# Routing counts from two products, the last block's two halves finished apart, and an express wait of block reads for all list stores

## The chip, the core and the metric

One core of a Trainium2 chip runs the whole program. The engines are named as the profile names them: PE (TensorE, the matrix products), PEld (the weight loads that belong to the products), DVE (VectorE), ACT (ScalarE), POOL (GpSimd) and SP (SyncE, which here only issues DMAs). The metric is the device time of one execution in microseconds (us), the median of several runs.

## What is computed

The input is x, 8 sequences of 512 tokens with 256 features. A modulation vector of each sequence gives shifts, scales and gates. Then:

```python
h = layernorm(x) * (1 + ca) + sa
x = x + ga * linear_attention(h)          # 16 heads of 16, causal, running sums
h = layernorm(x) * (1 + cb) + sb
x = x + gb * mixture_of_experts(h)

def mixture_of_experts(x):                # 8 experts, 256 -> 1024 -> 256
    probs = softmax(x @ router_w.T)
    topv, topi = top_k(probs, 2)          # two experts a token
    cw = weights of the two, normalised
    h = gelu(x @ w1[e]); y = h @ w2[e]    # only the two chosen matter
    return sum over e of cw[e] * y[e]
```

Everything is float32.

## The kernel before

**Two kinds of work.** For each of the 8 sequences, in chunks of 128 tokens, the attention part makes the normalised rows, the queries and keys, the causal sums and the new x (functions `early`, `middle`, `late`), and the rows that the experts will read (`rows_of`). After a sequence's four chunks `route` chooses each token's two experts. It counts, for each expert, how many earlier tokens chose it, and so knows the place ("slot") of each pair of token and expert in that expert's list. Then POOL stores each row into its slot in DRAM with an indirect DMA (`scatter`, line 963, 8 stores a sequence): these are the list stores. When lists are full enough, `plan` cuts blocks of 128 or 256 rows of one expert from them, as the table `TAKE` says (line 34), and after the last sequence `plan_rest` cuts all the rest.

**A block.** `fetch` issues three DMAs on SP: the expert's two weight matrices (lines 1216 and 1221, 1 MB each) and the block's rows from the lists (line 1227). `turn_rows` transposes the rows; `experts` computes the first layer group by group (`h_ps`), ACT applies the gelu (`g`), and `second` accumulates the second layer in one PSUM tile `y_ps`, which holds both 128-row halves of a block side by side. `finish` multiplies each half by the token's weight and gate on DVE (tile `y`) and has POOL add the half to its tokens' rows in DRAM with an indirect DMA (line 1321), into `acc`, or for the last blocks into the output itself. The last block of all is finished by `all_of` (line 1429), which calls `second` and `finish` once more when no further block follows.

**The order.** The program does not issue its work in the order of the source. Each piece is put into a planner (class `Plan`) with its engine, an estimated duration, a level (a lower one goes first) and what it reads and writes. `Plan.run` plays the work through with these estimates: each engine takes the ready piece of the lowest level. Expert blocks have levels from 1000 upwards, attention and routing lower ones, so that the experts' products fill what attention leaves free. The order that comes out is then issued as it stands, engine by engine; nothing is reordered on the chip. So an estimate that changes can change the order of other work, too. A group of products (`L.group("PE", us)`) is one piece, and its result counts as ready when the whole group is done.

**What the change touches.** In `route` (line 884): `is_in` holds 1 where an expert is among a token's two, for the four chunks of 8 experts each (128 x 32). The PSUM tile `at_ps` gets, by one product with the matrix `earlier`, the count of earlier tokens of the same chunk, and by four products with a matrix of ones the counts of the earlier chunks:

```python
for c in range(NC):
    product(
        at_ps[:, (c + 1) * E : (NC + 1) * E].rearrange("p (c e) -> p c e", e=E),
        ones, is_in[:, c, :].unsqueeze(1).to_broadcast([P, NC - c, E]),
        start=False, stop=(c == NC - 1), skip_group_check=True,
    )
```

DVE then makes the slots from it (`at`, `where`, `slot`) and adds the totals to `count`, from which `plan` and `plan_rest` work. In `second` and `finish` the halves of a block are one group and one piece of POOL's work. In `route`, `plan` and `plan_rest` the list `q.scatters` holds the stores of the one sequence just routed; a block's read waits for those.

Of the kernel before, what the change touches and what calls it, by code (L numbers as in the profile page):

```python
# [18 lines left out]
P = 128  # L19
# [319 lines left out]
def kernel(  # L339
# [60 lines left out]
    gathered = []  # L400
    added = []
    copied = []

    def apart(inst, others, why):
        for o in others:
# [478 lines left out]
    def route(q):  # L884
# [72 lines left out]
        dve(V.tensor_reduce, where, first, us=0.21, axis=AX.X, op=ALU.add)  # L957
        dve(V.tensor_copy, slot, where)
        dve(V.tensor_add, count, count, at_ps[:, NC * E : (NC + 1) * E])
        q.scatters = []  # L960

        def scatter(c, j):
            s = nc.gpsimd.indirect_dma_start(  # L963
                out=slots, out_offset=IndirectOffsetOnAxis(ap=slot.now()[:, c, j : j + 1], axis=0),
                in_=row.now()[:, c, :], in_offset=None,
                bounds_check=NONE - 1, oob_is_err=False,
            )
            apart(s, scattered + cleared, "a slot is of one pair of token and expert")
            apart(s, gathered, "blocks that are read are full by then")
            scattered.append(s)  # L970

        L.level += LEVEL["scatter"]
        for c in range(NC):
            for j in range(2):
                q.scatters.append(
                    L.do(
                        "POOL", 1.29, lambda c=c, j=j: scatter(c, j), r=[slot, row], landing=2.0,
                        mb=0.27,
                    )
                )  # L980
                q.scatters[-1].indirect = True


    def spans(small, n, tag):
# [294 lines left out]
            )  # L1279
        return block, w1_sb, w2_sb, xT, cw, to, r  # L1280

    def second(y_ps, w2_sb, nt, group, n_groups, each, g, level):

        L.level = level
        with L.group("PE", 0.433 * each * nt):
            for t in range(nt):
                for i in range(each):
                    product(
                        y_ps[:, ts(t, D)], g[:, i * nt * P + t * P : i * nt * P + (t + 1) * P],
                        w2_sb[:, each * group + i, :],  # L1290
                        start=(group == 0 and i == 0 and t == 0),
                        stop=(group == n_groups - 1 and i == each - 1), skip_group_check=True,
                    )

    def finish(block, cw, to, r, y_ps):
# [20 lines left out]
        def add():  # L1316
            halves = []
            for t in range(nt):
                if t:
                    nc.gpsimd.memset(between, 0.0)  # L1320
                s = nc.gpsimd.indirect_dma_start(  # L1321
                    out=out.rearrange("b s d -> (b s) d") if block.at_end else acc,
                    out_offset=IndirectOffsetOnAxis(ap=to.now()[:, t : t + 1], axis=0),
                    in_=y.now()[:, t, :], in_offset=None, compute_op=ALU.add,
                    bounds_check=TOK - 1 if block.at_end else TOK + 2 * P - 1,
                    oob_is_err=nt == 2 or not block.at_end,
                )
                apart(s, halves, "a token comes to an expert once")
                behind(s, added[-1:], "one addition to a token after the other")
# [3 lines left out]
            added.extend(halves)  # L1333

        X.adds.append(
            L.do("POOL", 1.85 * nt, add, r=[to, y], after=after, landing=2.0, mb=0.13 * nt)
        )
        X.adds[-1].indirect = True

    X.stores = []  # L1340

# [58 lines left out]
    for b in range(B):  # L1400
        if b not in xs:
            L.level = 4 * b - 12
            load_x(b, after=[X.stores[b - XS]] if b >= XS else ())
        L.level = 4 * b + LEVEL["open"]
        q = seqs[b] = open_(b, modded)
        for c in range(NC):
            for part, does in (("early", early), ("middle", middle), ("late", late)):
                L.level = 4 * b + c + LEVEL[part]
                does(q, c)
            L.level = 4 * b + c + LEVEL["rows"]  # L1410
            rows_of(q, c, modded)
# [90 lines left out]
```

## Time and profile before

| | us |
|---|---|
| median of 3 runs | 821.01 |
| the runs | 820.64, 821.01, 824.59 |
| the profiled execution | 827.9 |
| its span, first to last instruction | 826.2 |
| PE busy | 792.2 (96%) |
| weight loads busy | 658.3 (80%) |
| DVE busy | 378.0 (46%) |
| POOL busy | 320.6 (39%) |
| ACT busy | 284.3 (34%) |
| mean granted clock of TensorE | 0.985 |

All durations of instructions come from the one profiled execution. Its time is 1.7 us more than its span, and 6.9 us more than the median. In the page's 40 slices DVE is 70% busy or more from the second slice to about the twentieth (to some 400 us), and then a tenth; PE is at 80 to 90% and more in all but the first and last slices. So the program has an attention stage, in which both engines are loaded, and an expert stage, in which PE is nearly alone.

Each product of float32 matrices appears in the trace as two weight loads and two MATMUL instructions, so the 40 products on `at_ps` appear as 80 of each. Nearly all instructions bear line 220, the line of the planner's helper; they are told apart by the names of their tiles.

### The profile page before, as it was taken

What the parts mean: (1) busy time and instruction counts of PE and PEld (TensorE: products, weight loads), DVE (VectorE), ACT (ScalarE), POOL (GpSimd) and SP (SyncE); (2) the same over time, 40 slices, a digit from 0 to 9 for tenths busy, and PEclk for the clock granted to TensorE, in tenths of its full rate; (3) what the DMA queues carried; (4) which work ended last, traced back from release to release, by engine and by line L of the source; (5) the groups of instructions that cost most, each with busy time, mean ns of one, the idle gap of its engine ahead of it and who ended that gap; (6) DMA issues with size and microseconds to landing.
All of it is one profiled execution on the core that took longest, in us unless ns stands there. A gap on an engine that the chain in (4) does not pass through costs nothing. (4 is left out here: it accounts for less than half of the span.)

```text
span 826.2 us, 15967 instructions
## 1 busy us (share of the span) xinstructions
PE 792.2 (96%) x5998; PEld 658.3 (80%) x5998; DVE 378.0 (46%) x1290; ACT 284.3 (34%) x617; POOL 320.6 (39%) x477
## 2 busy tenths in 40 slices
PE   6899989999998999999999999999999999999995
PEld 3567657767786878789888888888988889898884
DVE  4588978888986888777263010111011111111000
ACT  2546444446464475552232122212221212222120
POOL 4734374637383364726138331312221232120133
PEclk9899998999998999999999999999999999999998
DMA  7320183964664353738579966766776878678932
GB/s 232 105 53 27 59 241 126 344 144 123 199 175 123 115 188 116 225 125 237 173 229 295 302 206 190 233 184 206 236 229 191 259 218 243 178 227 297 322 65 27
DMA packets 95167, 154.27 MB, mean 187 GB/s; under 512 B 6632, under 2 KB 69736, under 8 KB 94960
## 3 DMA queue, kind: packets, MB, share of 16 engines
q1 hardware_dynamic: 79680, 125.22, 48.5%
q0 software_dynamic: 15408, 28.00, 13.4%
q8 instruction: 49, 0.80, 0.4%
q14 instruction: 30, 0.25, 0.1%
HBM read 120.19 MB, written 37.20 MB: 191 GB/s over the span
## 5 line engine op out<-in xcount | busy, mean ns | idle before, releaser
L220 PE MATMUL h_ps<-xT,w 128*128 128x256 f32 (+1 forms) x1280 | 257.0, 351 | 2.6 <-issue 2.6
L220 PE MATMUL y_ps<-w,g 128*128 128x256 f32 x1072 | 253.7, 380 | 0.0
L220 PEld LDWEIGHTS h_ps<-xT,w 128*128 128x128 f32 x1280 | 216.3, 195 | 26.1 <-issue 3.2
L220 PEld LDWEIGHTS y_ps<-w,g 128*128 128x128 f32 x1072 | 200.2, 190 | 26.3 <-issue 0.8
L220 ACT ACTIVATE g<-h_ps 128x512 f32<-128x512 f32 x134 | 80.0, 597 | 309.0 <-PE h_ps L220 308.9
L1321 POOL DMA_INDIRECT acc<-y,to x57 | 90.2, 1582 | 243.8 <-DVE y L220 198.2
L220 DVE SCALAR_TENSOR_TENSOR y<-y_ps,cw,r 128x256 f32<-128x256 f32 x67 | 30.0, 480 | 154.6 <-PE y_ps L220 154.5
L220 DVE TENSOR_TENSOR sm<-s_ps,causal 128x512 f32<-128x512 f32 x128 | 82.3, 681 | 12.5 <-PE s_ps L220 12.5
L963 POOL DMA_INDIRECT slots<-row,slot x64 | 65.1, 1017 | 36.4 <-issue 13.1
L220 PE MATMUL qk_ps<-wqkv_sb,hT 128*128 128x512 f32 x128 | 65.1, 633 | 1.1 <-ACT hT L220 1.0
L220 DVE TENSOR_TENSOR cwe<-r,is_of_rest 128x16 f32<-128x16 f32 (+1 forms) x21 | 3.6, 174 | 132.6 <-DMA r<-slots 124.8
L220 POOL TENSOR_TENSOR f<-f,t 128x512 f32<-128x512 f32 x32 | 43.0, 1345 | 52.6 <-DVE t L220 41.5
L220 PEld LDWEIGHTS s_ps<-qT,kT 32*128 32x128 f32 x1024 | 32.6, 186 | 11.4 <-issue 7.3
L220 PE MATMUL s_ps<-qT,kT 32*128 32x128 f32 x1024 | 39.5, 284 | 1.5 <-ACT logits L220 0.7
L220 PEld LDWEIGHTS qk_ps<-wqkv_sb,hT 128*128 128x128 f32 x128 | 24.0, 202 | 20.3 <-issue 14.3
L220 PE MATMUL v_ps<-wqkv_sb,hT 128*128 128x256 f32 x128 | 36.2, 408 | 2.0 <-ACT hT L220 1.9
L220 PE MATMUL oT_ps<-sm,vz 128*32 128x128 f32 x1024 | 36.8, 276 | 1.3 <-DVE sm L220 1.2
L1321 POOL DMA_INDIRECT out_dram<-y,to x10 | 15.6, 1559 | 52.7 <-DMA out_dram<-acc 22.7
L220 POOL TENSOR_SCALAR mv_f<-mv_f 128x1 f32<-128x1 f32 x32 | 9.9, 310 | 64.8 <-DVE mv_f L220 59.3
L220 PE MATMUL a_ps<-wo,oT 128*128 128x256 f32 x128 | 33.6, 385 | 0.5 <-DVE sm L220 0.4
L220 ACT COPY xT<-x_ps 128x512 f32<-128x512 f32 (+1 forms) x40 | 20.6, 515 | 35.1 <-PE x_ps L220 34.8
L220 PEld LDWEIGHTS oT_ps<-sm,vz 128*32 128x32 f32 x1024 | 26.9, 109 | 6.7 <-DVE sm L220 3.2
(227 smaller groups left out, 1000.4 us busy)
## 6 DMA issues: line engine op xcount, KB each, us to landing
w<-in_w_dram SPq DMA_DIRECT2D x80, 1024.0 KB, 5.9
r<-slots SPq DMA_DIRECT2D x27, 521.0 KB, 7.0
row<-modd SPq DMA_DIRECT2D x8, 512.0 KB, 9.7
acc<-x SPq DMA_DIRECT2D x8, 512.0 KB, 3.7
out_dram<-acc SPq DMA_DIRECT2D x8, 512.0 KB, 9.0
x<-in_x_dram SPq DMA_DIRECT2D x7, 512.0 KB, 7.6
r<-slots SPq DMA_DIRECT2D x13, 260.5 KB, 8.7
mod<-modd SPq DMA_DIRECT2D x8, 384.0 KB, 6.3
```

What stands on the lines that cost most here:

```text
L220: return method(now(out), *[now(a) for a in args], **{k: now(a) for k, a in kw.items()})
L963: s = nc.gpsimd.indirect_dma_start(out=slots, out_offset=IndirectOffsetOnAxis(ap=slot.now()[:, c, j : j + 1], axis=0), in_=row.now()[:, c, ...
L1321: s = nc.gpsimd.indirect_dma_start(out=out.rearrange("b s d -> (b s) d") if block.at_end else acc, out_offset=IndirectOffsetOnAxis(ap=to.n ...
```

## The change

- `route`: DVE makes a second copy of `is_in`, called `up_to`, and adds up its chunks in place (one tensor_single_scalar and three tensor_add of 128 x 8 a sequence). The four products with `ones` become one product with `up_to`. The planner's estimate of the group goes from 1.05 to 0.45 us.
- `second` and `finish` get a flag `apart_`, set in `all_of` alone: the last block's last group of products becomes two groups, one for each half; DVE's product for a half follows that half's group, and each half's addition is a piece of POOL's work of its own that needs its own half of `y` alone. For other blocks the parts of `y_ps` are now named to the planner, in one group as before.
- A block's read names as its predecessors the list stores of all sequences so far (the list `scatters`), no longer those of the last sequence alone. Before, the older ones were declared independent of it.

```diff
@@ route
         dve(V.tensor_single_scalar, is_in, rank, 2.0, op=ALU.is_lt)
+        up_to = small([P, NC, E], "up_to")
+        dve(V.tensor_single_scalar, up_to, rank, 2.0, op=ALU.is_lt)
+        for c in range(1, NC):
+            dve(V.tensor_add, up_to[:, c, :], up_to[:, c - 1, :], up_to[:, c, :])
         at_ps = early_bank(f"at_ps_{b}")
-        with L.group("PE", 1.05):
+        with L.group("PE", 0.45):
             product(at_ps[:, : NC * E], earlier, is_in ...)
-            for c in range(NC):
-                product(
-                    at_ps[:, (c + 1) * E : (NC + 1) * E].rearrange("p (c e) -> p c e", e=E),
-                    ones, is_in[:, c, :].unsqueeze(1).to_broadcast([P, NC - c, E]),
-                    start=False, stop=(c == NC - 1), skip_group_check=True,
-                )
+            product(
+                at_ps[:, E : (NC + 1) * E], ones, up_to.rearrange("p c e -> p (c e)"),
+                start=False, stop=True, skip_group_check=True,
+            )
...
-        q.scatters = []
...
-                q.scatters.append(
+                scatters.append(
@@ second
-        with L.group("PE", 0.433 * each * nt):
-            for t in range(nt):
+        for halves in [[t] for t in range(nt)] if apart_ else [range(nt)]:
+            with L.group("PE", 0.433 * each * len(halves)):
+                for t in halves:
...
-                        y_ps[:, ts(t, D)], g[...]
+                        y_ps[:, ts(t, D)].of(t), g[...]
@@ finish
-                V.scalar_tensor_tensor, y[:, t, :].of(t), y_ps[:, ts(t, D)], cw[:, t, :],
+                V.scalar_tensor_tensor, y[:, t, :].of(t), y_ps[:, ts(t, D)].of(t), cw[:, t, :],
...
-        X.adds.append(
-            L.do("POOL", 1.85 * nt, add, r=[to, y], after=after, landing=2.0, mb=0.13 * nt)
-        )
-        X.adds[-1].indirect = True
+        for which in [[t] for t in range(nt)] if apart_ else [range(nt)]:
+            first = which[0] == 0
+            X.adds.append(
+                L.do(
+                    "POOL", 1.85 * len(which), lambda w=which, f=first: (add_first if f else add)(w),
+                    r=[to] + [y[:, t, :].of(t) for t in which], after=after if first else (),
+                    landing=2.0, mb=0.13 * len(which),
+                )
+            )
+            X.adds[-1].indirect = first
@@ the loop over sequences, and what follows it
-            blocks = plan(b, q.scatters)
+            blocks = plan(b, list(scatters))
...
-    blocks, others, more_i = plan_rest(q.scatters)
+    blocks, others, more_i = plan_rest(list(scatters))
...
-        second(*X.pending)
-        finish(*X.ending)
+        second(*X.pending, apart_=True)
+        finish(*X.ending, apart_=True)
```

More of the change, by code (lines that the diff above doesn't have):

```diff
@@ L402 @@
     copied = []
+    scatters = []
     def apart(inst, others, why):
@@ L970, in scatter @@
             scattered.append(s)
+            return s
         L.level += LEVEL["scatter"]
@@ L980, in route @@
                 )
-                q.scatters[-1].indirect = True
+                scatters[-1].indirect = True
     def spans(small, n, tag):
@@ L1280, in turn_rows, with second, finish @@
         return block, w1_sb, w2_sb, xT, cw, to, r
-    def second(y_ps, w2_sb, nt, group, n_groups, each, g, level):
+    def second(y_ps, w2_sb, nt, group, n_groups, each, g, level, apart_=False):
         L.level = level
-        with L.group("PE", 0.433 * each * nt):
-            for t in range(nt):
[L1287 to L1292, printed above, removed]
-                    )
-    def finish(block, cw, to, r, y_ps):
+        for halves in [[t] for t in range(nt)] if apart_ else [range(nt)]:
+            with L.group("PE", 0.433 * each * len(halves)):
+                for t in halves:
+                    for i in range(each):
+                        product(
+                            y_ps[:, ts(t, D)].of(t),
+                            g[:, i * nt * P + t * P : i * nt * P + (t + 1) * P],
+                            w2_sb[:, each * group + i, :],
+                            start=(group == 0 and i == 0 and t == 0),
+                            stop=(group == n_groups - 1 and i == each - 1), skip_group_check=True,
+                        )
+    def finish(block, cw, to, r, y_ps, apart_=False):
         n, nt = block.n, block.nt
@@ L1314, in finish, with add @@
         after = X.adds[-2:] + X.stores[-1:] + (X.copies or [])
-        def add():
-            halves = []
-            for t in range(nt):
+        halves = []
+        def add(which):
+            made = []
+            for t in which:
                 if t:
@@ L1328, in add @@
                 apart(s, halves, "a token comes to an expert once")
-                behind(s, added[-1:], "one addition to a token after the other")
+                behind(s, before_, "one addition to a token after the other")
                 if block.at_end:
@@ L1332, in add, with add_first @@
                 halves.append(s)
-            added.extend(halves)
-        X.adds.append(
-            L.do("POOL", 1.85 * nt, add, r=[to, y], after=after, landing=2.0, mb=0.13 * nt)
-        )
-        X.adds[-1].indirect = True
+                made.append(s)
+            if which[-1] == nt - 1:
+                added.extend(halves)
+            return made
+        before_ = []
+        def add_first(which):
+            before_.extend(added[-1:])
+            return add(which)
+        for which in [[t] for t in range(nt)] if apart_ else [range(nt)]:
[6 more added lines that the diff above has]
+                )
+            )
+            X.adds[-1].indirect = first
     X.stores = []
```

## The prediction

> **What bounds the kernel now.** I first read the busy shares on the page, then one row for each stretch of the span, to see where PE is full and where it isn't.
>
> ```profile
> PE 792.2 (96%) x5998; PEld 658.3 (80%) x5998; DVE 378.0 (46%) x1290; ACT 284.3 (34%) x617; POOL 320.6 (39%) x477
> ```
>
> ```profile
> 60.00:100.00 40.00, 37.85 (x468) 28.15 (x467) 37.02 (x98) 21.04 (x55) 14.02 (x18) 1.00 0.12 38
> 100.00:140.00 40.00, 35.79 (x337) 26.40 (x332) 33.82 (x123) 17.08 (x44) 24.76 (x40) 0.91 0.57 175
> 140.00:180.00 40.00, 38.41 (x453) 29.64 (x452) 31.92 (x87) 20.66 (x53) 21.29 (x32) 1.00 0.85 246
> 180.00:220.00 40.00, 39.35 (x432) 31.32 (x430) 35.22 (x122) 22.75 (x52) 24.09 (x36) 1.00 0.56 167
> 220.00:260.00 40.00, 39.01 (x436) 30.11 (x434) 30.95 (x114) 20.60 (x50) 21.62 (x33) 1.00 0.60 162
> 260.00:300.00 40.00, 37.37 (x362) 31.31 (x361) 30.35 (x102) 19.46 (x43) 22.19 (x35) 0.91 0.42 139
> ...
> 430.00:817.00 387.00, 387.00 (x1907) 342.23 (x1906) 53.87 (x251) 79.30 (x136) 102.43 (x138) 1.00 0.74 222
> ```
>
> The columns after the stretch are its length and the busy us of PE, PEld, DVE, ACT and POOL, then the granted clock and the DMA share. From 430 to 817 PE is busy all the time: 387.00 of 387. From 100 to 300 it idles 40 - 35.79 + 1.59 + 0.65 + 0.99 + 2.63, about 10 us in all, and the waits view names no single cause (the longest is 2.6 us). The experts' products fill what attention leaves. So the end is, to a few us, PE's work plus PE's idle time plus a tail: PE work taken out anywhere shortens the end, unless idle time takes its place. The chain of waits shows only the last addition on POOL and tells nothing of this.
>
> The price of the products on `at_ps` is read from the timeline of the weight loads at the last sequence's route, where PE is full on both sides:
>
> ```profile
> 424.04 1.70 PEld L220 LDWEIGHTS y_ps<-w,g 128*128 128x128 f32 x8
> 425.76 0.41 PEld L220 LDWEIGHTS at_ps<-is_in,earlier 128*128 128x128 f32 x2
> 426.09 0.97 PEld L220 LDWEIGHTS at_ps<-is_in,ones 128*128 128x128 f32 x8
> 426.98 1.60 PEld L220 LDWEIGHTS h_ps<-xT,w 128*128 128x128 f32 x8
> ```
>
> The reader is to see starts, not durations: five products (ten loads) hold the stream from 425.76 to 426.98, 1.22 us. Eight loads span 0.97, each lasts 0.192, so they start every (0.97 - 0.19) / 7 = 0.111 us. The moving matrix has 8 to 32 columns here, and the loads set the pace.
>
> **The change, part by part.** *Three products fewer a route.* Six load-and-product pairs x 0.111 = 0.67 us, x 8 routes = 5.3 us of PE. The other way, from the eight groups' whole stretches (1.11, 1.80, 1.43, 1.14, 1.32, 1.21, 1.32, 1.22, sum 10.55 for 80 pairs), six tenths of them are 6.3 us, but 1.80 lies partly in a stretch of half clock. I take 5.3. The one product that stays has 32 moving columns, as the widest of the four had.
>
> *Four DVE instructions more a route.* A tensor_single_scalar of 128 x 32 like `is_in` (176 ns) and three additions like `count` (152 ns), 0.63 us a route, 5.1 us in all. They depend on each other; dependent small instructions of this kind start 0.21 us apart (`red` at 421.11, 421.33, 421.54), so the chain to the products grows by up to 0.84 us, while the group that follows is 0.67 us shorter: the slots come 0.2 us later at worst. From the end of `is_in` to the first load of `at_ps` 1.40, 0.12, 0.26, 0.68, 1.27, 0.11, 0.86 and 2.34 us pass today; in four of eight the longer chain lies under a wait for PE, or nearly (0.86 is just enough). What hides DVE's time is the experts' backlog on PE. With that cover gone (PE behind DVE in each route) it costs 5.1 us. From below: nothing, where DVE waits for PE anyway (`x` for `a_ps` 24.2 us, `f` for `qk_ps` 12.6). DVE is densest around the routes: in the 8 us after the starts of five of the eight (96:104, 182:190, 225:233, 279:287, 327:335) it is busy 8.00 of 8, and PE idles 0, 0.65, 0.46, 0 and 0. By those five rows PE idles 1.1 us in 40 where DVE is full, so adding 5.1 us of DVE should cost little; I take 1.0 us, about a fifth, for this and for the new order together.
>
> *The new order.* The planner's estimates change, so other pieces may change places. PE has some 11 us of idle time left from the first route on. A new order can win part of that or lose as much; I count it at nothing with 2.5 us to either side, by the size of the longest single gap.
>
> *The wait for all stores.* An older sequence's stores were issued on POOL's queue before the new one's, and those the read already waits for; in the waits view SP stands at line 853 for `slots<-row,slot` (37.5 us, 6 times) earlier still, since the row tile is reused. The last store waited for is the same, so no read moves. What can grow is the number of waits. At the end of the program SP passes pairs of satisfied waits every 0.06 us; four such pairs for each of 40 reads make at most 10 us of SP. Behind a read stand the next block's weight loads and row load, the stores to `acc` and the loads of x; but SP has this to hide it:
>
> ```profile
> SPq L1216 <- PE h_ps L220: 216.4, 32, 19.4
> SPq L1221 <- PE y_ps L220: 96.5, 27, 4.6
> ```
>
> SP waits 216 us in total for PE to free first-layer weights, and PE has no wait for `r` at all. I take nothing. Without that cover a late block costs at most a read's 7.0 us. POOL issues as many stores and additions as before, ACT is not touched.
>
> *The tail.* The last half-block's products, DVE's two multiplications and POOL's two additions are in series:
>
> ```profile
> 813.70 3.43 PEld L220 LDWEIGHTS y_ps<-w,g 128*128 128x128 f32 x16
> ...
> 817.57 0.88 DVE L220 SCALAR_TENSOR_TENSOR y<-y_ps,cw,r 128x256 f32<-128x256 f32 x2 [11.21 <-PE y_ps L220]
> 818.33 1.55 POOL L1321 DMA_INDIRECT out_dram<-y,to  x1 [8.63 <-DVE y L220]
> 819.32 0.60 POOL L1320 MEMSET between<- 1x1 f32 x1
> 820.19 1.56 POOL L1321 DMA_INDIRECT out_dram<-y,to  x1 [0.27 <-POOLq L1453]
> ```
>
> The two multiplications take 0.48 each and 0.88 together, so the second starts 0.40 after the first. The first addition need no longer wait for it: 0.40 us. If DVE could also start when half of the last eight pairs is done (4 x 0.215 = 0.86 us), it would be 1.26 us; the second addition follows 1.86 us behind the first in any case, and its data come in time. No row here shows DVE reading a half of a PSUM tile while PE writes the other. Here the Trainium skill, page "PSUM — Partial Sum Buffer", section "PSUM bank collisions raise a hardware error", speaks against the change: two engines may not be in one bank at once, and the guard has to be by bank, not by address. `y_ps` is 512 float32 wide, one bank by that page. The second half's products come straight behind the first's on PE, so a guarded DVE still starts after both. By the rule 0.40, without it 1.26; I take 0.40.
>
> **The sum.** -5.3 + 1.0 + 0 - 0.4 = -4.7 us. On the profiled execution: 827.9 - 4.7 = 823.2. That execution is 6.9 us above the median, and the stretches show why it may be:
>
> ```profile
> 125.40:132.20 6.80, 5.66 (x70) 4.30 (x69) 6.20 (x25) 3.56 (x10) 2.19 (x3) 1.00 0.44 158
> 132.20:139.00 6.80, 6.80 (x29) 6.18 (x29) 6.49 (x30) 3.14 (x7) 2.62 (x5) 0.50 0.11 42
> ...
> 255.10:261.90 6.80, 4.52 (x58) 2.64 (x56) 3.17 (x9) 4.42 (x13) 2.40 (x5) 1.00 0.29 94
> 261.90:268.70 6.80, 5.92 (x28) 5.95 (x29) 4.38 (x8) 2.51 (x3) 2.94 (x3) 0.50 0.20 60
> ```
>
> Twice after the start PE had half its clock for 6.8 us, each worth about 3.4 us; two make 6.8. I read the two faster runs as having none of them and 824.59 as having one. Against the median the forecast is 821.0 - 4.7 = 816.3.
>
> **The rivals.** *The gain is filled by new idle time.* PE runs ahead sooner, and in the attention stage then waits for DVE, which has 5.1 us more to do and is full around the routes. Against it: the backlog, and the route of the last sequence lies where DVE is nearly idle. All of 5.1 us on the path gives 821.0 - 5.3 + 5.1 - 0.4 = 820.4; half gives 817.9.
>
> *Slower: the attention stage falls into half clock.* Place: the stretches from 84 to 270 in which PE is thin. With less PE work there and a denser DVE, more of them could be granted 0.50. Price: 3.4 us each. It decides from three more such stretches in the median run: 816.3 + 10.2 = 826.5. The skill, page "TensorE: Matmul & The Clock Gate", section "HAM oscillation — how this bites in real kernels", puts the rule as no idle gaps of PE above about 3.4 us. By it this rival is impossible, as PE's longest gap there is 2.6 us, and the sum stands. The rows say otherwise: half clock followed stretches with 5.66 and 4.52 of 6.80 busy and no gap over 2.6. But an earlier thin stretch, 84.41 to 91.24, with 5.30 us busy kept full clock, so the rows give no threshold either. The rows decide: possible, but three at once are unlikely, since 0.67 us less in one stretch of forty is little.
>
> *A lucky order.* The planner's new order also removes about 4 us of the 11 us of idle time: 812.3.
>
> *The change doesn't do what it says.* For the stores' wait I already take that as true. For the tail it would cost 0.4 us.
>
> **How the numbers follow.** A difference below 0.5%, 4.1 us, can't be told from none here: faster means below 816.9, slower above 825.1. The forecast as summed (814 to 818): 0.60; filled by idle time or by a single half-clock stretch (818 to 822): 0.23; three half-clock stretches or an order that loses as much: 0.09; a lucky order: 0.08. Of the first, four fifths are below 816.9, since the doubtful term (1.0 us for DVE) can also be nothing: 0.49 + 0.08 = 0.57 faster; 0.34 within; 0.09 slower. The range 811.5 to 822.0 leaves out the slow rival and a luckier order, with no more than 2 in 10.
>
> **What would show it.** Right: `at_ps` with 32 loads, groups of 0.4 to 0.6 us; PE's busy time lower by 5 us, its idle time from 100 to 430 up by 1 us or less; first addition of the last block 0.4 us closer to the last product, not 1.26; SP's waits for PE still above 200 us. Wrong: waits of PE for `sm`, `row` or `f` that grow by more than 3 us; a wait of PE for rows; or a different number of 0.50 stretches, which would move the profiled time by 3.4 us each.

## The result, and the profile after

| | before | after |
|---|---|---|
| median, us | 820.89 (22 runs, 817.48 to 825.51) | 824.71 (22 runs, 820.64 to 826.97) |
| ratio of after to before | | 1.0037, 95% interval 1.0021 to 1.0052 |
| the profiled execution, us | 827.9 | 825.43 |
| its span, us | 826.2 | 823.7 |
| its mean granted clock | 0.985 | 0.984 |

The kernel became slower by 0.37%. That is less than the half per cent below which the prediction saw no change, but the forecast of 816.3 and its range up to 822.0 are missed, and the sign is wrong. (Ratios stand here as they were recorded, with their intervals; a quotient of two medians can differ from them by some 0.3%.) The two profiled executions say the opposite of the medians: after is shorter by 2.5 us. Both happen to have nearly the same clock. So what can differ between the medians and not between these two profiles is how often an execution is granted the full clock.

First the busy time of the changed kernel, from its page:

```profile
PE 787.6 (96%) x5950; PEld 651.9 (79%) x5950; DVE 386.2 (47%) x1322; ACT 286.4 (35%) x619; POOL 317.1 (38%) x476
```

PE has 24 products fewer (48 MATMULs and as many loads) and 4.6 us less work. The weight loads of the last route, from the timeline of after, show where it went (start, duration, instruction):

```profile
433.06 0.41 PEld L220 LDWEIGHTS at_ps<-is_in,earlier 128*128 128x128 f32 x2
433.39 0.30 PEld L220 LDWEIGHTS at_ps<-up_to,ones 128*128 128x128 f32 x2
433.74 0.30 PEld L220 LDWEIGHTS h_ps<-xT,w 128*128 128x128 f32 x2
```

Four loads hold the stream for some 0.67 us where ten held it for 1.22. Over the eight routes the stretches are 0.92, 0.54, 0.68, 0.87, 0.76, 0.36, 0.44 and 0.67 us, 5.24 in place of 10.55, so 5.31 us less.

The stretches of the attention stage (length; busy us of PE, PEld, DVE, ACT, POOL; granted clock; DMA share and GB/s):

```profile
100.00:140.00 40.00, 36.05 (x368) 26.86 (x367) 34.17 (x124) 17.34 (x45) 23.45 (x39) 0.91 0.51 170
...
260.00:300.00 40.00, 39.11 (x440) 30.88 (x439) 32.52 (x114) 21.95 (x55) 19.49 (x31) 1.00 0.49 152
300.00:340.00 40.00, 36.29 (x391) 27.79 (x393) 31.40 (x104) 17.51 (x42) 16.12 (x25) 0.91 0.44 112
```

The stall that before had after 255 is gone, and another of the same kind stands at 300 to 340. All gaps of over 60 ns in which neither PE nor its loads are busy, after 20 us, add up to 17.7 us before and 20.0 after: 2.3 us of the 5.3 are given back as idle time.

What that stall is, the timeline of after shows:

```profile
319.04 0.17 DVE L220 TENSOR_TENSOR cwe<-r,is_of 128x8 f32<-128x8 f32 x1 [3.52 <-DMA r<-slots]
...
319.29 0.68 DVE L220 TENSOR_TENSOR sm<-s_ps,causal 128x512 f32<-128x512 f32 x1
...
320.03 1.91 PE L220 MATMUL oT_ps<-sm,vz 128*32 128x128 f32 x26 [2.79 <-DVE sm L220]
```

`cwe` is an instruction of 0.17 us that makes the weights of a later expert block from that block's rows. It stands at the head of DVE's queue, its rows are not there, and DVE idles 3.52 us with it. The attention's `sm` is ready behind it and can't pass; PE waits 2.79 us for `sm`. Before has a like picture at 257.8, where `cwe` waits 4.88 us; PE's gap of 2.63 us follows at 260.2, and its row names no releaser. Half clock comes behind the stall, here in after at two places:

```profile
128.10:131.50 3.40, 1.20 (x13) 0.63 (x7) 1.21 (x6) 1.34 (x5) 0.39 (x1) 0.99 0.58 190
131.50:134.90 3.40, 3.40 (x18) 3.40 (x17) 3.40 (x16) 1.86 (x3) 0.00 (x0) 0.50 0.02 5
...
312.40:319.20 6.80, 4.83 (x54) 2.85 (x47) 2.83 (x6) 2.89 (x8) 1.83 (x4) 1.00 0.96 306
319.20:326.00 6.80, 5.97 (x38) 4.84 (x39) 5.31 (x15) 1.55 (x5) 1.26 (x1) 0.50 0.03 11
```

Each thin stretch is granted the full clock, and the one behind it, in which PE is busy again, half. A third half-clock stretch of after, from 117.8 to 121.2, follows one in which PE was busy for 6.18 of 6.90 us, so a long gap is not needed. Between 100 and 430 us both profiles have 13.6 us at half clock.

The tail in after:

```profile
811.36 3.62 PE L220 MATMUL y_ps<-w,g 128*128 128x256 f32 x16
815.01 0.88 DVE L220 SCALAR_TENSOR_TENSOR y<-y_ps,cw,r 128x256 f32<-128x256 f32 x2 [11.21 <-PE y_ps L220]
815.77 1.56 POOL L1329 DMA_INDIRECT out_dram<-y,to  x1 [8.62 <-DVE y L220]
```

From the start of the multiplications to the first addition 0.76 us pass, exactly as before (817.57 to 818.33). The tail gained nothing.

And SP's queue still waits for PE, in the view of its waits (us in all, times, longest):

```profile
SPq L1220 <- PE h_ps L220: 206.7, 32, 20.6
```

### The profile page after: what moved, and what is told of

The parts are those of the page before. It is cut to its first block, busy times and chain, and to the rows that moved or that the text cites. A ratio compares the mean times of both kernels' runs of the same rounds, so it can differ in the third digit from the quotient of the medians.

```text
span 823.7 us, 15905 instructions
## 1 busy us (share of the span) xinstructions
PE 787.6 (96%) x5950; PEld 651.9 (79%) x5950; DVE 386.2 (47%) x1322; ACT 286.4 (35%) x619; POOL 317.1 (38%) x476
## 5 line engine op out<-in xcount | busy, mean ns | idle before, releaser
L220 PE MATMUL h_ps<-xT,w 128*128 128x256 f32 (+1 forms) x1280 | 254.0, 348 | 1.0 <-ACT xT L220 0.5
L220 PEld LDWEIGHTS h_ps<-xT,w 128*128 128x128 f32 x1280 | 213.3, 192 | 24.9 <-issue 0.8
```

The costliest lines, as they stand in the source:

```text
L220: return method(now(out), *[now(a) for a in args], **{k: now(a) for k, a in kw.items()})
```

## The experiments

Times are told as ratios to before, timed on the same chip. The kernels e5 to e8, and e9, e10, e12 and e13, ran on two chips where every kernel, before and after alike, took some 48 us longer; there only ratios are read. "Late" below means that the small DVE instructions that need a block's rows (`cwe`, `cw`, `to`), for the blocks of the attention stage, stand just ahead of their first reader.

**e1: the new counts in before's order.** All five DVE instructions and both products bear before's estimates, so that the planner gives the order of before.

```diff
-        dve(V.tensor_single_scalar, is_in, rank, 2.0, op=ALU.is_lt)
+        with L.group("DVE", 0.15 + 0.00104 * is_in.free):
+            ...is_in, up_to and the three additions as in after
         with L.group("PE", 1.05):
             ...the two products of after
```

> The new counts (two products, four more DVE instructions a route) issued in exactly the order of the kernel before; the tail and the stores' wait as before. Theory ORDER (the loss comes from the planner's new order, the new counts by themselves save about 5 us of PE): about 816, ratio to before 0.993 to 0.996; PE idle time from 20 to 430 within 1.5 us of that of before. Rival DVE (the four DVE instructions a route, on a full DVE, cost more than the products save): 823 to 825, ratio above 1.002.

Measured: 824.13 us, ratio 1.0011 (0.9991 to 1.0032). The counts alone bring nothing in the old order. Apart from the counts' own instructions every engine has the same sequence as in before, so the two profiles can be matched load by load. At 437 us the PE of e1 is 7.1 us ahead. But 3.9 of it are won from 128 to 140 and 4.9 from 256 to 270: there before has its two half-clock stretches, and at the second place a stall of 2.6 us; this execution has neither half clock, and a stall of 1.5. Outside these places e1 is 1.7 us behind before. At five routes (near 96, 182, 224, 279 and 326) a lead of 0.2 to 0.7 us appears and is lost again within 5 us; they are the five behind which DVE is busy for 8.00 of 8 us in before. At the last two (near 375 and 426), where it is busy for 7.17 and 6.77 of 8, 0.65 and 0.67 us stay. PE's waits for DVE's `sm` and `row` show where it goes (us in all, times, longest), in before

```profile
PE rt_ps L220 <- DVE row L220: 1.9, 3, 1.1
PE oT_ps L220 <- DVE sm L220: 1.2, 6, 0.3
PE rt_ps L220 <- DVE sm L220: 1.0, 2, 0.6
PE a_ps L220 <- DVE sm L220: 0.4, 1, 0.4
```

and in e1

```profile
PE rt_ps L220 <- DVE row L220: 2.4, 4, 1.1
PE oT_ps L220 <- DVE sm L220: 2.1, 7, 0.8
PE rt_ps L220 <- DVE sm L220: 1.8, 4, 0.6
PE a_ps L220 <- DVE sm L220: 1.6, 3, 0.7
```

together 4.5 and 7.9 us. From 437 to 462, where the last sequence hands over to the experts, e1 loses another 4.3 us:

```profile
444.77 0.17 DVE L220 COPY to<-r 128x2 int32<-128x2 int32 x1 [10.58 <-DMA acc<-y,to]
...
445.81 1.72 PE L220 MATMUL y_ps<-w,g 128*128 128x256 f32 x4 [2.35 <-issue]
```

Again a small DVE instruction (`to`, the tokens' places) heads the queue, now until an addition to `acc` has landed, and the multiplication that frees `y_ps` stands behind it. Half clock for 3.4 us follows.

**e2: the old counts in after's order.** The five products stay; the planner is told of after's estimates.

```diff
+        up_to = small([P, NC, E], "up_to")
+        L.do("DVE", 0.15 + 0.00104 * up_to.free, lambda: None, r=[rank], w=[up_to])
+        for c in range(1, NC):
+            L.do("DVE", 0.15 + 0.00104 * E, lambda: None, r=[up_to], w=[up_to])
-        with L.group("PE", 1.05):
+        with L.group("PE", 0.45) as counts:
+            counts.reads.append(up_to)
```

> The old five products and no DVE instruction more, but issued in the order that the changed kernel has (the planner is told of the new durations and of four pieces of DVE work that issue nothing); the tail and the stores' wait as before. Theory ORDER: slower than before by what the change lost plus what its products saved, 827 to 830, ratio 1.007 to 1.011; DVE again stands before a late block's rows near 130 and near 319, and PE with it. Rival DVE: as before, ratio 0.998 to 1.002.

Measured: 830.96 us, ratio 1.0090 (1.0058 to 1.0123). Its products and DVE's instructions are those of before, and apart from the counts every engine has the sequence of after (with it come two table loads more on ACT and one memset fewer on POOL). With the old counts this order costs 0.9%, 7.4 us. DVE stands before the rows of a block for 5.33 us at 323, and PE 4.50 us with it, where after's stall at 319 took 2.79. After holds the same order and the new counts, at 1.0037: the counts save 0.5%, 4.4 us, in this order, though the two were not timed side by side (with e16 below it is 0.8%).

**e3: the tail and the stores' wait alone.**

```diff
-            blocks = plan(b, q.scatters)
+            blocks = plan(b, list(scatters))
...
+        second(*X.pending, apart_=True)
+        finish(*X.ending, apart_=True)
```

> The change without its counts: the last block's halves apart and the reads' wait for all stores, five products as before; no engine's order differs from before. Theory ORDER and rival DVE: no difference, ratio 0.998 to 1.002; the first addition of the last block again begins 0.76 us after the first half's multiplication, so the tail gives nothing. Rival WAIT (the express wait delays the reads): 823 to 825, ratio above 1.002, and reads that land later than before.

Measured: 824.01 us, ratio 0.9990 (0.9961 to 1.0020): nothing. The first addition again follows 0.76 us behind the multiplications' start. PE, DVE and POOL do the same instructions with the same number of waits as in before; of the 40 reads of rows four have another number of waits.

These runs gave something else. The program hardly differs from before, and its 14 runs lie apart: six at a mean granted clock of 0.995 with 818.2 to 819.2 us, eight at 0.985 to 0.989 with 823.5 to 827.5. So runs of one program lie some 6 us apart, and the clock goes with the time. The section on the prediction uses this.

**e4: after, with the rows' instructions late and the modulation's loads behind the reads.**

```diff
+    def move(order):
+        ...each of cwe, cw, to of an attention-stage block: just ahead of its first reader
+        ...each load of mod that stands on SP just ahead of a read of rows: behind it
+        return order
+        L.order = move(L.order)
```

> The changed kernel with two moves in the issued order: the three small DVE instructions that need a block's rows stand as late as their users allow (attention-stage blocks only), and two modulation loads on SP stand behind the row reads instead of ahead of them. Theory ORDER, in its form that a late row read at the head of an in-order queue is what thins PE out and brings half clock: DVE's waits for rows before 430 go from 5.7 us to below 1, PE's longest gap after 100 falls below 1.5 us, the half-clock stretches near 131 and 319 are gone, 816 to 820, ratio to before below 1.000. Rival DVE: as the changed kernel, ratio 1.002 to 1.005.

Measured: 823.47 us, ratio 1.0003 (0.9981 to 1.0024). The stall at 319 is gone. (A half clock of 3.4 us remains near 330, behind 4 us in which PE is busy for 2.04 with no gap over 0.73.) But the load of `mod` that was moved is now what is late:

```profile
128.76 0.69 DVE L220 TENSOR_TENSOR wo<-wout_sb,mod 128x512 f32<-128x512 f32 x1 [3.31 <-DMA mod<-modd]
...
129.93 2.07 PE L220 MATMUL s_ps<-qT,kT 32*128 32x128 f32 x26 [3.28 <-DVE x L220]
```

One late transfer was exchanged for another at the same place.

**e5: after, late only.** The first half of that edit.

> The changed kernel with one move alone: the small DVE instructions that need a block's rows (cwe, cw, to) as late as their users allow, for the attention-stage blocks; SP's order as in the changed kernel. Theory HEAD OF QUEUE (a small instruction that waits for a DMA holds an in-order engine, PE goes thin, half clock follows): DVE waits for rows before 430 fall from 5.7 to below 0.5 us, PE's gap of 2.8 near 317 and the half clock at 319 go; the gap near 129 stays, since PE itself waits for the rows there. Time below the changed kernel by 2 to 6 us: 819 to 823, ratio to before 0.998 to 1.002. Rival CHANCE (half clock comes whatever the queues do): as the changed kernel, 1.002 to 1.005.

Measured: 873.12 us, ratio 1.0041 (1.0021 to 1.0060), where after gave 1.0037 on another chip: no gain seen. (A later run beside after on one chip corrects this.)

**e6: e1 with more buffers for `to`.**

```diff
-        to = L.tile(pb, [P, 2], "to", f"to_{n}", 3, I32)
+        to = L.tile(pb, [P, 2], "to", f"to_{n}", 6, I32)
```

> The new counts in the old order, and the tile of the rows' targets (to) has six buffers, not three, so that its copy on DVE need not wait for an older addition to land. Theory HEAD OF QUEUE: DVE's wait of 10.6 us for an addition near 434 to 445 and PE's gap of 2.3 at 443 go; the 7 us that the new counts are ahead by there are kept up to the slack of the first block of the rest (4 us), so PE then runs 4 to 7 us ahead of before; 816 to 819, ratio 0.994 to 0.998. Rival HANDOVER (the rest's first rows land when the last stores do, whatever PE does): PE waits for rows near 460 instead, ratio 0.999 to 1.003.

Measured: 877.88 us, ratio 1.0093 (1.0069 to 1.0118; 6 runs). Slower, not faster. The waits of `to` for an addition, 27.9 us in all in e1, are gone in this profile; PE's longest gap at the handover is now 3.7 us, near 499, behind ACT's `g`. So that the wait of `to` is what loses time there is not shown. What the buffers do by themselves is not known, since e1 did not run on this chip.

**e7: before, late.** The `move` above on before, without the loads of `mod`.

> The kernel before with the same one move (cwe, cw, to as late as their users allow, attention-stage blocks), five products, nothing else. Theory HEAD OF QUEUE: DVE's wait of 4.9 us for rows at 258 goes, and with it PE's gap of 2.6 at 260 and the half clock at 262: 815 to 819, ratio 0.993 to 0.998. Rival CHANCE: as before, 0.999 to 1.002.

Measured: 865.79 us, ratio 0.9950 (0.9928 to 0.9971; 7 runs). Faster than both kernels.

**e8: e6, late.**

> The new counts in the old order with both remedies: six buffers for the targets, and cwe, cw, to late for the attention-stage blocks. Theory HEAD OF QUEUE: the best of all, 813 to 817, ratio 0.990 to 0.996, no half clock between 100 and 430. Rival HANDOVER: not below e7, since what is gained ahead of 430 is lost at the first block of the rest: ratio 0.996 to 1.000, with a wait of PE for rows near 460.

Measured: 869.47 us, ratio 0.9992 (0.9963 to 1.0020). Late is worth 0.9992/1.0093, 1.0%, on top of e6; yet e8 stays 0.4% behind e7, before with late and the old counts.

**e9 and e10: the planner told that rows land after 6 us, not 2,** in after and in before. The reads of rows take 7.0 to 8.7 us from issue to landing on the pages of both kernels.

```diff
-        L.do("SP", 0.6, rows, r=[block.slot], w=[r], after=block.seen, landing=2.0, mb=0.26 * nt)
+        L.do("SP", 0.6, rows, r=[block.slot], w=[r], after=block.seen, landing=6.0, mb=0.26 * nt)
```

> The changed kernel with one number more: the planner is told that a block's rows land 6 us after their issue, not 2 (measured from issue to landing: 7.1 median, 5.6 to 10.9), so it makes another order again. Theory ESTIMATE (the order holds engines at rows that have not landed since the planner expects them too early): DVE's waits for rows before 430 below 1 us, no gap of PE above 1.2 us between 100 and 430 that ends with the landing of rows, below the changed kernel of the same chip by 3 to 7 us, ratio to before 0.993 to 0.999. Rival CHANCE (one order is as good as another, only luck decides): ratio anywhere from 1.000 to 1.006.

> The kernel before with the same one number (rows land after 6 us, not 2), five products. Theory ESTIMATE: DVE's wait of 4.9 at 258 goes; below before by 1 to 5 us, ratio 0.994 to 0.999, and e9 below it by 3 to 5 us, what the products save. Rival CHANCE: 0.998 to 1.005 and no fixed distance to e9.

Measured: after 883.0 us, ratio 1.0149 (1.0111 to 1.0188); before 874.34 us, 1.0042 (1.0027 to 1.0057). The theory that a truer estimate would mend the order fell in both. DVE's waits for rows before 430 us did become short (1.8 us in e9, where after has 3.0 on that chip, and 0.7 in e10), but the time rose; PE's longest waits there are now for ACT's `oT`, 4.6 and 7.8 us. A changed estimate makes a new order for everything.

**e12 and e13: after again, and e7 again,** on the same chip as these two.

> The changed kernel itself once more, on the chip of the other kernels here, as their common measure. Both theories: ratio to before 1.002 to 1.005; hardly a run with a mean clock of 0.993 or more, where before has a quarter of its runs there.

> The kernel before with cwe, cw, to as late as their users allow (as in e7), once more on this chip. Theory HEAD OF QUEUE: ratio 0.993 to 0.998 as in e7, no PE gap of 2.6 near 260 and no half clock there. Rival CHANCE: e7 was luck of its chip, 0.999 to 1.002.

Measured: after 875.59 us, 1.0062 (1.0042 to 1.0082); before with late 868.32 us, 0.9969 (0.9952 to 0.9985). After is slower than before here too, and before with late faster.

**e14 to e16: the order's price without waits for rows.** The kernel with old counts in after's order and late as well (e14), after with late (e15, the kernel of e5) and after (e16), all on one chip, where before takes 823.8 us.

> Before with its five products a route, issued in the order of after (as e2), but cwe, cw and to of the attention stage's blocks stand on DVE just ahead of their first reader, as in e7. Theory ROWS (the order's price of 0.9% in e2 is the wait of DVE for rows in the attention stage): the ratio falls from 1.009 to that of e7, 0.995 to 0.998. Theory SPREAD (most of the order's price lies elsewhere: the handover at 430 to 465, PE's waits for other things): ratio 1.004 or more.

> e5 once more, beside after on the same chip. Theory ROWS: faster than after by 0.4% or more, near 0.999 of before. Theory SPREAD: within 0.2% of after, 1.003 to 1.006 of before, as e5 had it. Its ratio to e14 is the worth of the counts in one order without waits for rows: 0.994 if the three products fewer are on the path there, 1.000 if what is saved is lost again.

> After itself, as the measure for e14 and e15 on this chip: 1.0037 to 1.0062 of before by its other runs.

Measured: e14 825.79 us, 1.0033 (1.0015 to 1.0052); e15 820.09 us, 0.9971 (0.9954 to 0.9988); e16 823.74 us, 1.0009 (0.9994 to 1.0025). e14 lies between what the two theories expected: set against e2, on another chip, late takes away 0.57% of 0.9%, and something is left. Between e14 and e15 the counts differ (and the tail and the stores' wait, which brought nothing in e3): 0.9971/1.0033 = 0.9938, 5.1 us. And late does help after, by 0.38%; e5 had been compared with after on another chip.

**e11: the tail with two PSUM banks.** Before, the last block's second half in a bank of its own, its products a group of their own.

```diff
-        with L.group("PE", 0.433 * each * nt):
...
+        for part in parts:
+          with L.group("PE", 0.433 * each * len(part)):
...
+            y_ps = [y_ps, late_bank(f"y2_ps_{n}") if final else y_ps]
```

> Before with only the last block's halves changed: two groups of products in two PSUM banks, each multiplied when its own group is done. Theory BANK (in after DVE waits for both halves since they share a bank): DVE's first multiplication starts about 0.86 us earlier against the last product than in before, so its start lies ahead of the last product's end; the first addition follows it by 0.5 to 0.8 us, and the end of the span comes about 0.9 us nearer to the last product. Theory QUEUE (DVE or POOL is bound by something else, such as its own start-up): nothing moves.

Measured, in the timeline of this kernel:

```profile
810.44 3.62 PE L220 MATMUL y_ps<-w,g 128*128 128x256 f32 x16
813.23 0.48 DVE L220 SCALAR_TENSOR_TENSOR y<-y_ps,cw,r 128x256 f32<-128x256 f32 x1 [10.35 <-PE y_ps L220]
813.99 1.55 POOL L1323 DMA_INDIRECT out_dram<-y,to  x1 [7.76 <-DVE y L220]
814.09 0.48 DVE L220 SCALAR_TENSOR_TENSOR y<-y_ps,cw,r 128x256 f32<-128x256 f32 x1 [0.38 <-PE y_ps L220]
```

The last products end at 814.06. DVE's first multiplication starts 0.83 us ahead of that, where in before it starts 0.04 behind; the first addition comes 0.07 ahead, where it came 0.80 behind. The addition is 0.87 us nearer to the last product, and that is the 0.86 us that the prediction had worked out for a DVE that needn't wait for the second half. By the semaphores in the traces the wait is one of the program: in before and after only the last of the 16 MATMULs signals to DVE, here also the last one of the first half, which ends at 813.19. That fits the theory of the bank; but the edit gives the second half another tile and another bank at once, and does not tell the two apart.

**e17 and e18: both repairs in after, and e7 once more,** on one chip with before at 821.93 us.

> After with cwe, cw and to of the attention stage's blocks just ahead of their first reader (e15), and the last block's second half in a PSUM bank of its own (e11). By e15 0.9971 of before, and 0.87 us less by e11: 0.996. If the tail's gain is lost (a second bank that something else wanted), 0.997.

> Before with cwe, cw and to late, alone (e7), on the same chip as e17. If the planner's order costs more than waits for rows (e14 at 1.0033 against 0.995 to 0.997 here), this stays at 0.995 to 0.997, level with e17, and the counts' 5 us are what the order takes back. If e7 owed its gain to the slower chip it ran on, 0.999 or more, and then the waits are the order's whole price.

Measured: e17, after with late and two banks, 820.43 us, 0.9982 (0.9966 to 0.9997); its first addition again comes 0.07 us ahead of the last product's end, but 0.1% is too little to see in the ratio. e18, before with late: 816.74 us, 0.9934 (0.9910 to 0.9957; 6 runs at a clock of 0.993 to 0.995). It is the fastest kernel of the study, 0.66% under before, with the same instructions in another order. With late in both orders and the old counts, after's order costs 1.0033/0.9934 = 1.010 (about 1.007 to 1.013 from the two intervals; 1.008 and 1.006 with e7 and e13 in place of e18), much as without late. So waits for rows are an item of their own, which before and after both pay, and not the price of the order.

What the order loses with the old counts and late, the stretches of the two kernels show at one place. First e14, in after's order, then e18, in before's:

```profile
100.00:140.00 40.00, 36.26 (x366) 26.87 (x362) 32.88 (x115) 17.26 (x45) 22.67 (x37) 0.91 0.53 163
...
119.00:122.40 3.40, 3.40 (x7) 1.83 (x6) 3.31 (x7) 0.36 (x1) 2.19 (x5) 0.56 0.44 138
...
129.00:132.40 3.40, 1.15 (x8) 0.75 (x7) 3.40 (x13) 1.43 (x4) 0.02 (x1) 0.98 0.55 197
132.40:135.90 3.50, 3.50 (x20) 3.50 (x19) 0.28 (x1) 2.08 (x3) 0.00 (x0) 0.53 0.02 5
```

```profile
100.00:140.00 40.00, 36.41 (x393) 27.78 (x392) 35.69 (x127) 19.21 (x51) 25.72 (x43) 1.00 0.55 190
```

PE is busy for nearly the same time in both, but in e14 at half clock for some 7 us of it. In the thin stretch from 129.0 to 132.4 PE waits 1.75 us for the first block's rows. SP's queue and the product in after, which has the same order there:

```profile
119.07 0.34 SPq L656 DMA_DIRECT2D mod<-modd  x1
...
120.95 0.35 SPq L1231 DMA_DIRECT2D r<-slots  x1
```

```profile
130.41 0.41 PE L220 MATMUL x_ps<-ident,r 128*128 128x128 f32 x2 [1.74 <-DMA r<-slots]
```

In after's order the load of the next sequence's `mod` stands ahead of the first block's read of rows on SP and issues only at 119.07; the read follows at 120.95. In before the `mod` load comes behind it (121.51), and the read issues at 118.54, in before with late at 116.82. But this sets e14 apart from e18, and not after from before: before's own row for 100 to 140 us has 0.91 too, with half clock from 132.2 to 139.0 behind no gap above 0.7 us, although its read stands ahead of `mod`. The rest of the price is spread: over the whole span PE's gaps of over 60 ns add up to 20.4 us in e14 and 17.1 in e18, and the mean clock over the runs is 0.987 against 0.994.

The stalls themselves can be followed through the profiles of the chips where before takes 821 to 824 us. Before, e3 and e11 all have the stall of 2.6 us near 260, and half clock begins within 1 us of its end. In e18, with late, there is neither. After, e16 and e2 have the stall near 318 and half clock at its end in the same way. In e4, e14, e15 and e17, with late, that stall is gone; in e14 and e15 no half clock follows, in e4 and e17 3.4 us of it come near 330 and 327.

## Why the prediction was wrong

**The step that failed: that the products' time, once off PE, comes off the end, with 1.0 us given back for DVE and the new order counted "at nothing with 2.5 us to either side".** The prediction said itself that PE work shortens the end "unless idle time takes its place". The ratios to before show that it does, in either order:

| | old counts | new counts |
|---|---|---|
| before's order | 1 | 1.0011 (e1) |
| after's order | 1.0090 (e2) | 1.0037, and 1.0009 in e16 |

In before's order the counts were to bring -5.3 + 1.0 = -4.3 us. They brought +0.9 (-0.7 to +2.6): PE's waits for DVE's `sm` and `row` grew by 3.4 us there, and the handover took more. That is the rival "filled by new idle time", which had 0.23 together with a single half-clock stretch. With the old counts, after's order costs 7.4 us, three times the bound that was set for a new order. The two do not add up: +0.9 and +7.4 would make 1.010, and the change has 1.0009 to 1.0037. With the new counts the two orders lie between no difference and 0.3% apart. So 7.4 us is not what the order took from the change; it is the price of that order for the old counts.

A rival that no run tests is that a mixed pair pays for being mixed: e1 and e2 each run one kind of counts in an order that was planned for the other. It would fit the kernels with late: the pairs that belong together have 0.9934 to 0.9969 (e18, e7, e13) and 0.9971 (e15), the mixed ones 0.9992 (e8, which also has six buffers) and 1.0033 (e14).

**Idle time and the clock.** The bound on the order was the size of PE's longest gap, as if an order could lose only a gap. It can also lose the clock. Over the 102 runs of before on two chips the time falls by 0.75 us for each 0.001 of mean granted clock. That is near what half clock alone would cost: 6.83 us of it lower the mean by 0.0042 and cost at most 3.4 us, 0.82 us for each 0.001. By this line:

| kernel | mean clock of its runs | before's on that chip | difference by the clock, us | the rest, us |
|---|---|---|---|---|
| e1: new counts, before's order | 0.9911 | 0.9902 | -0.7 | +1.4 |
| e2: old counts, after's order | 0.9843 | 0.9902 | +4.4 | +4.7 |
| e14: the same, late | 0.9873 | 0.9896 | +1.7 | +0.5 |
| e16: after | 0.9882 | 0.9896 | +1.0 | -0.6 |
| e15: after, late | 0.9899 | 0.9896 | -0.3 | -2.5 |
| e18: before, late | 0.9940 | 0.9903 | -2.8 | -2.6 |

(Differences of the means over the runs, which for e2 make 9.1 us where its ratio makes 7.4; the line is a fit, and the split an estimate from it.) The profiles agree where their clocks do: e2 at 0.984 has a span 5.0 us longer than before at 0.985, and 5.3 us more gaps. For after itself the line leaves 0.6 us of gain at an equal clock and takes 1.0 us by the clock. Before reaches a clock of 0.993 or more in 14 of 58 runs on that chip, and after in none of 22 (in the first comparison in one of 22). Between e14 and e18 the rest differs by 3.1 us, near the 3.2 us by which their gaps differ. With late in both, before and after have the same rest, -2.6 and -2.5: PE's gaps from 20 us on are 14.8 us in e18 and 18.9 in e15, so by these two profiles idle time took back 4.1 us of what the products saved.

**Three products fewer: 5.3 us. Right as work on PE.** It is 5.31 us by the stretches, and 4.6 by PE's busy time. As time it depends on the order: nothing in before's (e1), and 5.1 us in after's with late (e14 and e15), of which the line puts 2.0 to the clock, so that some 3 are left.

**Four DVE instructions more: 1.0 us taken. Too small.** The prediction saw the five stretches in which DVE is full and took 1.0 us from PE's idle time there as it was. By e1, with the order kept, the whole saving was given back, and at just these five the lead was lost. DVE's busy time rose by 8.2 us, not 5.1, but only 2.5 of it belong to the counts (387.1 in e15 against 384.6 in e14); DVE's busy time with the old counts and late is 384.6 in after's order and 378.7 in before's.

**The reading of the median.** "I read the two faster runs as having none of them", the half-clock stretches, is right in kind and not in size: before's runs at a clock of 0.995 on one chip take 818.7 us on the mean of seven, some 2 us less than the 820.64 and 821.01 that were read as free of half clock. Before's low times rest on a full clock, and a new order can take that away. The rival that named half clock as the mechanism asked for three more stretches and got 0.09. The profile has no more of them than before's, and by the line the clock's part in after is 1.0 us.

**The rule on the clock.** The Trainium skill's page "TensorE: Matmul & The Clock Gate", section "HAM oscillation — how this bites in real kernels", gives as its abstract rule that PE should have no idle gaps above about 3.4 us; taken as the only way to half clock, it would let none follow a shorter gap. In after half clock follows gaps of 2.79 and 1.74 us, in e1 one of 2.35. The rows decide, as the prediction said.

**"PE has no wait for r at all", the cover for the reads. The line was true and the conclusion wrong.** PE waits for `sm`, `sm` for its turn on DVE, and the head of DVE's queue for rows. By what late gains, this costs 0.31 to 0.66% in before and 0.38% in after. The listed sign "a wait of PE for rows" did appear (1.74 us). The waits of `oT_ps` for `sm` grew from 1.2 to 4.0 us, just short of the 3 us named as a sign.

**The wait for all stores: nothing. Right**, by e3 and by SP's 206.7 us of waits for PE.

**The tail: 0.40 taken. Wrong.** The first addition already waited for its own half only: 0.76 us from the multiplications' start, less than their 0.88 together. The row that said so was in the prediction's own fence, 817.57 and 818.33. The upper end, 1.26, was rightly left out: the page "PSUM — Partial Sum Buffer", section "PSUM bank collisions raise a hardware error", has accesses guarded by bank and not by address. The traces agree: with both halves in one bank DVE starts 0.04 us behind the last product, with two banks 0.83 us ahead of its end.

**What stays open.** Whether the order or its mismatch with the counts costs the time is not settled, and e1's loss at the handover is not traced to a cause. The 4.4 us that the counts save in after's order are themselves the difference of after and e2, so that they and e2's 7.4 us make up after's +3.0 proves nothing; with the 5.1 us of e14 and e15 the sum is +2.3. The first comparison gave 3.0 us and e16 0.7, so the loss itself is good to a few us only.

## What to carry to other kernels

When an edit changes a planner's estimates, run the old work in the new order and the new work in the old order before you credit or blame either, and then see whether the two effects add: here they did not. Look at what stands at the head of each in-order queue waiting for a transfer: an instruction of 0.17 us that nobody needs soon held up the whole attention chain, and moving it back won 0.3 to 0.7%. Read the granted clock of every run before comparing medians, and bound a new order's risk by gaps and by the clock together.

## What was not expected of the hardware

Half clock came after stalls of PE of 1.7 to 4.5 us, and in e4 without any gap over 0.73, after a stretch in which PE was half idle. One program with one order runs at a mean clock of 0.985 or of 0.995 from run to run, 6 us apart. On two other chips the same kernels took some 48 us longer (before: 869.6 and 870.3 us), with a mean clock of 0.955 to 0.976. The page of after there has its clock row as

```profile
PEclk9999888798999997979999999999999999999998
```

with PE gaps in clusters, the longest a wait of 6.8 us for ACT (`xT`) and one of 5.5 us for `oT`; its gaps from 20 us on add up to 50.0 us, where after has 20.0. What holds ACT there was not found.
